# Two graph layers on one core: layernorm scaling and GAT slope on ScalarE, whole runs of weighted sums, packed loads, a second GAT block beside the first, and a timed instruction order

## Chip, cores and metric

One core of one Trainium2 chip. The metric is the device time of one execution in microseconds (us), median of the runs. TensorE is "PE" in the profile, its weight load "PEld", VectorE "DVE", ScalarE "ACT", GpSimd "POOL". SBUF is the on-chip memory that all engines use, PSUM the one that TensorE writes its results to.

## The reference, cut to what matters

128 graphs of 128 nodes with 256 features pass through two layers, all in fp32.

```python
# layer 0: two graph-attention (GAT) blocks, then a feed-forward
def _gat(h, adj, W, a):
    Wh = h @ W
    e = leaky_relu(Wh @ a[:F] + swapaxes(Wh @ a[F:], 1, 2), 0.2)
    att = softmax(where(adj > 0, e, NEG), axis=1)
    return att @ Wh
h = layernorm(x + gat(gat(x)))            # g, b
h = layernorm(h + relu(h @ wf1 + bf1) @ wf2 + bf2)
# layer 1: 8 heads, 4 relations; each relation r weighs its own values
attn = softmax(q @ k.T / sqrt(32))
out = sum((attn * (adj == r)) @ v_r for r in range(4))
x = layernorm(h + out @ Wo + bo)
x = layernorm(x + gelu(x @ W1 + b1) @ W2 + b2)
```

In the data every gain is 1 and every bias 0. The kernels compute with them all the same.

## The kernel before

It works on groups of four graphs, 32 groups. Each group has five stages (load, GAT, feed-forward 0, attention, feed-forward 1), written as Python generators. A loop takes the steps of many groups in turn by a nominal time, so that one group's attention stands beside another's feed-forwards. The program is then put in order for each engine by a scheduler that follows this sequence, and each engine executes its own list in order.

```python
def layernorm(y, k):                     # all on VectorE but the power
    for b in range(G):
        nc.vector.bn_stats(st, y[:, b]); nc.vector.bn_aggr(mv[:, b], st)
    nc.vector.tensor_scalar(rstd, mv[:, :, 1], EPS, None, op0=OP.add)
    nc.gpsimd.tensor_tensor(rstd, rstd, mhalf, OP.pow)
    g, beta = ln[k]                      # rows, the same in all partitions
    for b in range(G):
        nc.vector.scalar_tensor_tensor(y[:, b], y[:, b], mv[:, b, 0:1], g, op0=OP.subtract, op1=OP.mult)
    for b in range(G):
        nc.vector.scalar_tensor_tensor(y[:, b], y[:, b], rstd[:, b:b + 1], beta, op0=OP.mult, op1=OP.add)

def feed_forward(h, ...):
    hT = transposed(h)                   # PE transposes, copies by ACT and DVE
    yield
    nc.gpsimd.tensor_add(y, h, over_graphs(bout))     # bias of its second product, 128x1024
    # ... cut: matmuls, eviction with the activation on ACT, second matmuls

def gat_weighting(wh, c, cap):
    # ... cut: four PE transposes into p
    nc.vector.tensor_tensor(e, p, wh[:, :, c:c + 1].to_broadcast([P, G, N]), OP.add)
    nc.vector.scalar_tensor_tensor(e, e, ALPHA, e, op0=OP.mult, op1=OP.max)
    nc.vector.scalar_tensor_tensor(e, cap, BIG, e, op0=OP.subtract, op1=OP.min)
    # ... cut: row maximum, four Exp on ACT, reciprocal, product on POOL

def weighted(ms, v):                     # "av": 32 matmuls, 32 output rows each
    for c in range(DC):
        for r in range(R):
            for q in range(HC):
                nc.tensor.matmul(po[ts(q, DH), c], v[:, r, ...], ms[c][r][:, q],
                                 start=r == 0, stop=r == R - 1, tile_position=(0, q * DH))

# loads: first group, then weights; 25 of them, 18 small vectors and 7 pieces of matrices, are issued by ACT
stages = ((stage_load, 1, -0.7, -0.6), (stage_gat, 6, 0.0, 0.5), (stage_ff0, 7, 0.65, 1.15),
          (stage_attention, 15, 2.0, 3.0), (stage_ff1, 7, 3.15, 3.65))   # steps, begin, end
```

Names in the lines below: `tr` is a transpose into PSUM, `T` its copy in SBUF, `mm` any other product, `wh` the GAT projection, `e` the weights of a GAT block or of attention, `kbd` the keys as the score product reads them, `v` the values, `m` the masked weights, `av` the weighted sum, `cap` the GAT mask, `fT` the hidden layer of a feed-forward. Each fp32 matmul shows as two instructions.

## Time and profile before

3866.5 us. Cut by the first wq matmul of each group, the profiled execution is:

| stretch | us | floor of TensorE's work in it | idle of TensorE, up to its last matmul |
|---|---|---|---|
| start, up to the second group's wq | 243.6 | 149.6 | 67.4 |
| 28 full periods, mean | 117.5 | 107.5 | 5.1 |
| the rest | 332.7 | 282.8 | 24.5 |

"Floor" is the sum of the start-to-start times that each kind of matmul has in an unbroken run (0.43 us for 512 columns, 0.216 for 256, 0.109 for a transpose, 1.89 for the 64 instructions of an av block), worked out as the prediction tells.

In the start, ScalarE's first work waited for its own load issues, and the GAT chain ran alone. From the timeline of the kernel before (start, length, engine, line, operation, count, idle before and releaser):

```profile
27.35 1.28 ACT L236 ACT_TABLE_LOAD   x1 [27.35 <-DMA wv<-in_wv_dram]
```

```profile
40.32 3.81 PE L244 MATMUL mm<-wh,e 128*128 128x258 f32 x8 [9.93 <-POOL e L224]
...
50.88 3.69 PE L253 MATMUL mm<-wh,e 128*128 128x256 f32 x8 [5.97 <-POOL e L224]
59.31 2.11 PE L160 MATMUL tr<-ident,tok 128*128 128x128 f32 x8 [4.74 <-issue]
61.67 15.43 PE L193 MATMUL mm<-T,wf 128*128 128x512 f32 x32 [0.25 <-ACT T L164]
```

Each GAT matmul waits for a chain over DVE, ACT and POOL; the first feed-forward (L193) begins at 61.7 us.

### The profile page before, as it was taken

Reading aid. Unit: us, or ns where it says so; the run is one execution under the profiler, and the core shown is the slowest. Engines: PE = TensorE matmul, PEld = TensorE weight load, DVE = VectorE, ACT = ScalarE, POOL = GpSimd, SP = SyncE. Lnnn points to the kernel's source line nnn. Section 1 sums busy time; section 2 is a strip of 40 time slices with the busy share of each in tenths; the row PEclk is TensorE's granted clock in tenths of the full one; section 3 lists DMA queues with packets and bytes.
Section 4 is the critical chain, followed back from the end, with each engine's and each line's share of the span. In section 5 each row is a group of like instructions: output and inputs, shape, how many; then the busy total and the mean of one; then the engine's idle time right before and its main releaser. Section 6 shows DMA issues by size and latency. Waiting matters only on the chain.

```text
span 3866.8 us, 51771 instructions
## 1 busy us (share of the span) xinstructions
PE 3623.2 (94%) x20240; PEld 2329.2 (60%) x20240; DVE 2236.5 (58%) x4804; ACT 1509.9 (39%) x4272; POOL 722.4 (19%) x552
## 2 busy tenths in 40 slices
PE   5799999999999999999999999999999999999998
PEld 3456666566565665666665656665656665656655
DVE  2466565655656556555666565566565566565654
ACT  1243444434444334453334443334443334443342
POOL 0121111211112112111111122111122111122111
PEclk8899999999999999999999999999999999999999
DMA  4000000000000000000000000000000000000000
GB/s 160 8 9 20 14 17 9 20 20 15 20 6 20 20 15 20 6 20 20 20 14 20 6 20 20 20 14 20 6 20 20 20 15 14 6 9 6 6 7 11
DMA packets 28884, 70.83 MB, mean 18 GB/s; under 512 B 5600, under 2 KB 11616, under 8 KB 28640
## 3 DMA queue, kind: packets, MB, share of 16 engines
q1 hardware_dynamic: 21328, 63.19, 4.7%
q10 hardware_dynamic: 7312, 4.34, 0.4%
q8 instruction: 159, 2.61, 0.3%
q14 instruction: 85, 0.70, 0.1%
HBM read 50.74 MB, written 16.78 MB: 17 GB/s over the span
## 4 chain that ended last, share of the span: by engine, by line
PE 68%; DVE 17%; ACT 9%; issue 3%; POOL 2%; DMA 1%; ACTq 0%; POOLq 0%; DVEq 0%; SPq 0%
PE mm L203 22%; PE mm L193 17%; PE mm L319 6%; DVE m L310 5%; PE av L330 4%; DVE tok L181 3%; ACT kbd L280 3%; PE mm L287 3%; PE mm L266 3%; PE mm L353 2%; PE mm L244 2%; PE mm L276 2%; PE tr L306 2%; PE mm L235 1%; PE tr L160 1%
## 5 line engine op out<-in xcount | busy, mean ns | idle before, releaser
L310 DVE SCALAR_TENSOR_TENSOR m<-at,tr 128x512 f32<-128x512 int32 x1024 | 631.0, 680 | 5.8 <-PE tr L306 5.1
L204 DVE TENSOR_TENSOR tok<-tok,mm 128x512 f32<-128x512 f32 x128 | 88.0, 687 | 781.8 <-PE mm L203 781.8
L319 PE MATMUL mm<-wv,T 128*128 128x512 f32 x1024 | 479.8, 603 | 0.0
L193 PE MATMUL mm<-T,wf 128*128 128x512 f32 x1024 | 469.3, 600 | 6.8 <-DVE T L162 6.3
L193 PE MATMUL mm<-T,w 128*128 128x512 f32 x1024 | 470.0, 602 | 2.0 <-ACT T L164 0.5
L293 ACT ACTIVATE e<-mm,nm 128x128 f32<-128x128 f32 x1024 | 360.3, 372 | 266.0 <-DVE nm L289 162.6
L203 PE MATMUL mm<-w,fT 128*128 128x256 f32 x2048 | 455.5, 381 | 0.0
L203 PE MATMUL mm<-wf,fT 128*128 128x256 f32 x2048 | 452.4, 379 | 0.0
L203 PEld LDWEIGHTS mm<-w,fT 128*128 128x128 f32 x2048 | 386.6, 190 | 71.1 <-issue 21.5
L203 PEld LDWEIGHTS mm<-wf,fT 128*128 128x128 f32 x2048 | 386.7, 190 | 51.3
L295 POOL TENSOR_TENSOR e<-e,s 128x512 f32<-128x512 f32 x256 | 276.9, 1082 | 702.6 <-DVE s L294 700.0
L176 POOL TENSOR_TENSOR rstd<-rstd,mhalf 128x4 f32<-128x4 f32 x128 | 150.9, 1179 | 1369.9 <-DVE rstd L175 1369.9
L280 ACT ACTIVATE kbd<-mm,bk 32x256 f32<-32x256 f32 x512 | 238.3, 465 | 376.2 <-PE mm L276 365.0
L181 DVE SCALAR_TENSOR_TENSOR tok<-tok,rstd,lnb 128x256 f32<-128x256 f32 x512 | 292.9, 624 | 104.6 <-POOL rstd L176 104.6
L195 ACT ACTIVATE fT<-mm,bf 128x512 f32<-128x512 f32 x256 | 175.4, 694 | 413.1 <-PE mm L193 412.0
L193 PEld LDWEIGHTS mm<-T,wf 128*128 128x128 f32 x1024 | 192.2, 191 | 229.4 <-issue 203.1
L193 PEld LDWEIGHTS mm<-T,w 128*128 128x128 f32 x1024 | 191.3, 193 | 230.1 <-issue 205.1
L330 PEld LDWEIGHTS av<-m,v 128*32 128x32 f32 x8192 | 219.0, 109 | 155.4 <-issue 99.9
L330 PE MATMUL av<-m,v 128*32 128x128 f32 x8192 | 286.5, 275 | 13.7 <-DVE v L320 13.4
L287 PE MATMUL mm<-kbd,T 128*128 128x512 f32 x512 | 257.8, 606 | 24.0 <-ACT kbd L280 24.0
L319 PEld LDWEIGHTS mm<-wv,T 128*128 128x128 f32 x1024 | 183.6, 194 | 158.9 <-issue 158.5
L289 DVE TENSOR_REDUCE nm<-mm 128x4 f32<-128x512 f32 x256 | 173.5, 683 | 175.6 <-PE mm L287 175.6
(65 smaller groups left out, 4243.0 us busy)
## 6 DMA issues: line engine op xcount, KB each, us to landing
xt<-in_xT_dram SPq DMA_DIRECT2D x32, 512.0 KB, 3.3
tok<-in_x_dram SPq DMA_DIRECT2D x32, 512.0 KB, 3.2
out_dram<-tok SPq DMA_DIRECT2D x32, 512.0 KB, 2.6
at<-in_adjT_dram SPq DMA_DIRECT2D x32, 256.0 KB, 2.6
wf<-in_wf_dram SPq DMA_DIRECT2D x2, 1024.0 KB, 8.9
w<-in_w_dram SPq DMA_DIRECT2D x2, 1024.0 KB, 9.3
wv<-in_wv_dram ACTq DMA_DIRECT2D x2, 512.0 KB, 9.9
lng<-in_g_dram ACTq DMA_DIRECT2D x4, 128.0 KB, 6.0
```

What stands on the lines that cost most here:

```text
L181: nc.vector.scalar_tensor_tensor(y[:, b], y[:, b], rstd[:, b:b + 1], beta, op0=OP.mult, op1=OP.add)
L193: nc.tensor.matmul(p, win[:, c, ts(f, P)], hT[:, c], start=c == 0, stop=c == DC - 1)
L195: nc.scalar.activation(t, p, func, bias=bin_[:, f:f + 1])
L203: nc.tensor.matmul(p[:, b - b2_], fT[f][:, ts(b, N)], wout[:, f], start=f == 0, stop=f == FC - 1)
L280: nc.scalar.activation(kbd[c][rows, :, q], p[rows], AF.Identity, bias=bk[rows, c:c + 1])
L287: nc.tensor.matmul(p, qT[:, c, ts(b, N)], kbd[c][:, b % KG], start=True, stop=True)
L289: nc.vector.tensor_reduce(nm, p, AX.X, OP.max, negate=True)
L293: nc.scalar.activation(e[:, q], p[:, q], AF.Exp, bias=nm[:, q:q + 1], accum_out=s[:, q:q + 1])
L295: nc.gpsimd.tensor_mul(e, e, per_row(s, N))
L310: nc.vector.scalar_tensor_tensor(m, ab, r, pT, op0=OP.is_equal, op1=OP.mult)
L319: nc.tensor.matmul(p, hT[:, f, ts(b, N)], wv[:, f, r:r + 2], start=f == 0, stop=f == DC - 1)
L330: nc.tensor.matmul(po[ts(q, DH), c], v[:, r, c * P + q * DH:c * P + (q + 1) * DH], ms[c][r][:, q], start=r == 0, stop=r == R - 1, tile_pos ...
```

## The change

The intent: relieve VectorE, keep the narrow matmuls together, and shorten the start.

```diff
-    # bcast(), cols(): one small load for each vector, on nc.scalar's queue
+    # COLS, rows: all vectors packed into `cols` and `rows`; every load on nc.sync,
+    # in the order M, W2T, xT[0], W1T, adj[0], x[0], cols, wf1, rows, wf2, ... w2, then group 1
     # normalised(), was layernorm()
-        for b in range(G):  # two VectorE passes with row vectors g, beta
-            nc.vector.scalar_tensor_tensor(... subtract mean, times g)
-            nc.vector.scalar_tensor_tensor(... times rstd, plus beta)
+        nc.vector.scalar_tensor_tensor(nmr, mv[:, :, 0], -1.0, rstd, op0=OP.mult, op1=OP.mult)
+        for b in range(G):
+            nc.scalar.activation(y[:, b], y[:, b], AF.Identity, bias=nmr[:, b:b + 1], scale=rstd[:, b:b + 1])
+    def affine(y, k, b):     # gain, then offset with the next bias, two graphs at a time, off the path
+        for op, v in zip((OP.mult, OP.add), ln[k][0]):
+            nc.gpsimd.tensor_tensor(y[:, b:b + 2], y[:, b:b + 2], v[:, None, :].to_broadcast([P, 2, D]), op)
     # transposed(): gain and offset go into the copies, where they are per partition
-                nc.vector.tensor_copy(t[:, c], p)
+                nc.vector.tensor_scalar(t[:, c], p, gain[:, c:c + 1], offset[:, c:c + 1], op0=OP.mult, op1=OP.add)
     # gat_weighting()
+        for b in range(G):
+            nc.scalar.activation(p[:, b], p[:, b], AF.Prelu, bias=wh[:, b, c:c + 1], alpha=ALPHA)
-        nc.vector.tensor_tensor(e, p, wh..., OP.add)
-        nc.vector.scalar_tensor_tensor(e, e, ALPHA, e, op0=OP.mult, op1=OP.max)
-        nc.vector.scalar_tensor_tensor(e, cap, BIG, e, op0=OP.subtract, op1=OP.min)
+        nc.vector.scalar_tensor_tensor(e, cap, BIG, p, op0=OP.subtract, op1=OP.min)
     # weighted(): last mask first, so the first matmul's wait covers all, and a higher priority
-            for c in range(DC):
-                for r in range(R):
+            with tc.high_priority(offset=200):
+                for c in reversed(range(DC)):
+                    for r in reversed(range(R)):
     # attention(): keys(b + 1) one step earlier; every yield now has a share of its stage's time
-        att = gat_weighting(wh, D + 2, cap)
-        yield
+        att = gat_weighting(wh, D + 2, cap)
+        yield 4
+            if g == 1 and n < 2:         # the second group's load and GAT beside the first's
+                begin, end = begin - 0.6, end - 0.6
-    with tile.TileContext(nc) as tc:
+    with tile.TileContext(nc, schedule_with_timeline_sim=True) as tc:
```

The last line hands the order of instructions to a scheduler that works with estimated durations ("timed scheduler" below).

## The prediction

> **What bounds the kernel now.** I read the page first, then busy time by stage, the order of work on TensorE inside one stage, and what the other engines did in its gaps. From the page, busy time, share of the span and instruction count:
>
> ```profile
> PE 3623.2 (94%) x20240; PEld 2329.2 (60%) x20240; DVE 2236.5 (58%) x4804; ACT 1509.9 (39%) x4272; POOL 722.4 (19%) x552
> ```
>
> TensorE (PE) is the bound; the others have 40% or more to spare on average. So work moved between VectorE, ScalarE and GpSimd can only help through the idle 243 us of TensorE, and through time in which it is "busy" but stretched.
>
> Stage table. The first wq matmul of each group of four graphs (L266) marks a period. Columns: window, length, busy time by engine (PE, weight load, DVE, ACT, POOL), granted clock, DMA share, GB/s.
>
> ```profile
> 150.76:243.55 92.79, 84.84 (x529) 53.59 (x528) 59.56 (x130) 33.06 (x118) 19.35 (x15) 0.98 0.03 9
> 243.55:359.60 116.05, 111.25 (x634) 71.55 (x633) 70.33 (x150) 46.35 (x133) 22.60 (x17) 1.00 0.05 17
> 359.60:480.10 120.50, 114.99 (x634) 74.02 (x633) 70.04 (x150) 49.29 (x135) 22.60 (x17) 0.97 0.05 16
> 480.10:598.70 118.60, 113.14 (x634) 73.09 (x633) 70.06 (x150) 49.30 (x135) 22.60 (x17) 0.99 0.05 16
> 3739.30:3867.00 127.70, 106.61 (x585) 64.70 (x583) 57.67 (x131) 38.88 (x107) 17.72 (x14) 0.95 0.02 9
> ```
>
> The kernel is a start of 150.8 us, one short period of 92.8, 29 like periods up to 3648.4 (mean 117.4; either 116.0 at clock 1.00, or 120.5 and 118.6 in turn at 0.97 and 0.99), and an end of 90.9 + 127.7. The reader is to see that equal work costs up to 4.5 us more where the clock dips.
>
> One undisturbed period on TensorE (start, length, line, operation, count, idle before it and its releaser):
>
> ```profile
> 2605.81 3.60 PE L266 MATMUL mm<-T,wq 128*128 128x512 f32 x8
> ...
> 2610.97 7.07 PE L203 MATMUL mm<-wf,fT 128*128 128x256 f32 x32
> 2617.88 1.92 PE L235 MATMUL mm<-wx,xt 128*128 128x260 f32 x8
> ...
> 2626.34 0.65 PE L213 MATMUL tr<-ident,wh 128*128 128x128 f32 x4 [2.24 <-DVE T L162]
> ...
> 2629.84 0.65 PE L306 MATMUL tr<-ident,e 128*128 128x128 f32 x4 [1.31 <-POOL e L295]
> ...
> 2661.15 0.84 PE L330 MATMUL av<-m,v 128*32 128x128 f32 x18
> 2662.45 1.13 PE L287 MATMUL mm<-kbd,T 128*128 128x512 f32 x2 [0.45 <-ACT kbd L280]
> 2663.50 0.64 PE L330 MATMUL av<-m,v 128*32 128x128 f32 x16
> ...
> 2691.71 1.95 PE L330 MATMUL av<-m,v 128*32 128x128 f32 x64
> ```
>
> Start-to-start rates of unbroken runs give a floor: 32 at 256 columns take 6.91 us (0.216 each), those of 512 columns 0.43, a transpose 0.109, the 64 narrow av matmuls 1.89. Times the counts of a period: two feed-forwards 55.1, values 13.7, scores 6.9, q and k 6.9, wo 3.5, av 7.6, GAT 7.0, transposes 7.0: **107.5 us**. The clean period is 116.0, so 8.5 us are lost: 4.8 idle, 3.7 stretched.
>
> The longest wait is DVE's copy L162. What DVE and POOL did ahead of it:
>
> ```profile
> 2622.46 2.34 POOL L188 TENSOR_TENSOR tok<-tok,b 128x1024 f32<-128x1024 f32 x1 [0.97 <-PE tr L160]
> 2622.53 2.56 DVE L181 SCALAR_TENSOR_TENSOR tok<-tok,rstd,lnb 128x256 f32<-128x256 f32 x1
> ...
> 2625.61 0.68 DVE L162 COPY T<-tr 128x512 f32<-128x512 f32 x1
> ```
>
> One layernorm instruction whose median is 0.48 us took 2.56, for as long as POOL's bias add. Everything behind it on DVE slid, the T copy too, and TensorE stood still.
>
> **What the Trainium skill says.** "SBUF — State Buffer", section "Who interferes with whom": a DVE instruction with two SBUF inputs contends with a GpSimd instruction that reads SBUF, as an exclusive lock for the whole instruction; with at most one SBUF input (outside two-port modes) it does not. The trace agrees: L181 reads tok and lnb from SBUF and has 447/480/2566 ns as minimum, median, maximum. "TensorE: Matmul & The Clock Gate", Part 1, says the clock halves after low activity in a window of about 3.4 us; the 0.97 and 0.99 periods agree in kind. "ScalarE: Activation LUTs", "What ACT_TABLE_LOAD costs": 1283 ns a load, which the trace shows exactly (1283), 186 ns plus 0.833 per element for an ACTIVATE, some 93 ns for each pointer operand, and about 93 ns overlap between neighbours. "Trainium Kernel Development and Optimization", "Key Constraints": loads issued from several engines share the same 16 DMA engines. In the first 50 us they were 90% busy at 302 GB/s, so one queue loses no bandwidth; it frees ScalarE's sequencer, whose first copy had waited until 27.35 us behind its own load issues.
>
> **The change, part by part.** (Counts from the built kernel's order of instructions.)
>
> 1. *Matmul work:* counts are identical, so the floor of 107.5 stays.
> 2. *DVE.* Removed: both layernorm passes (292.9 + 267.9 us) and two of the three GAT passes (43.6 + 51.4) = 655.8. Added: 128 tiny products (21) and slightly dearer transpose copies (7). 2236 becomes about 1610 us. More important: the remaining full-width DVE operations read one operand from PSUM or have one SBUF input, so the lock should disappear from DVE.
> 3. *ACT.* Added: 512 scalings of 256 elements, about 0.46 us each back to back (estimate from L280, 465 ns, and the ScalarE page's pointer and overlap terms) = 235; 256 Prelu of 128 elements at about 0.3 = 80; dearer transpose copies 17. Table loads fall from 208 to 184, −31. 1510 becomes about 1810 (50%). Not a bound.
> 4. *POOL.* Removed: 96 bias adds, 225.7. Added: 512 operations on 128x512 at about 1.08 (row L295 has 1082 ns on that size) = 553. 722 becomes 1050 (29%). These sit on residual data, off the path to the next matmul, since gain and offset go into the transpose copies.
> 5. *Order on TensorE.* The 32-matmul av blocks (64 instructions) become unbroken, keys are issued earlier, and a timed scheduler fixes the rest.
>
> Taken back from the clean period's 8.5: the T wait 2.4, the POOL wait before L306 1.5, the GAT matmul waiting and running slow (L244) 1.1, broken av runs with their kbd waits 1.5: 6.5. The remaining 2.0 is about 0.1 us at each change of matmul kind, which stays. That makes 109.5 at best; I choose **111.0**, adding 1.0 for new waits of an in-order ScalarE or POOL with more to do and 0.5 for clock dips. 29 × (117.4 − 111.0) = 186 us.
>
> *Start.* The chain of waits there is serial GAT work, twice: TensorE waits 11.9, 6.6, 9.9, 6.0, 4.7 in group 0 and 8.6, 6.1, 4.6 in group 1. Now M, W2T, xT and W1T come first (1.3 MB, some 4 us at 302 GB/s plus 2 of latency); the first GAT can run about 10 us sooner. But the second group's xT is queued behind all weights: 10.6 MB, about 37 us, and its projection stands ahead of group 0's last GAT matmul. So group 0's feed-forward starts at about 53 us, not 61.7. From there to the first wq, 58 us of work is dense: 3% for changes and 3 for a cold clock make 62. First wq at **115** instead of 150.8: −36. The next stretch has similar gaps to lose: 92.8 to **87**, −6.
>
> *End.* The last feed-forward has no neighbour. The final normalisation gains two POOL operations per half after ScalarE, partly overlapped: about +4. The attention before it loses its broken av runs, −3.5. 218.6 becomes **219**.
>
> Sum: 115 + 87 + 29 × 111.0 + 219 = 3640 us, 5.9% shorter.
>
> **Rivals.** (a) *ScalarE becomes the wait.* One normalisation is now four scalings of 0.46 in an in-order stream that also holds eight kbd writes (3.9 us in a row), feed-forward evictions and table loads. With four mm buffers, TensorE would stall at L193 or L287. For it: kbd already shows as a releaser. Against: 50% load, and a stream ordered for it. Two such waits of 1.5 us a period make 114, total near 3725. (b) *POOL, with the lock now against itself or with 2.2 us pairs in front of the attention product L295.* POOL already held 2.35 us operations, so I expect no more; at 1 us in each of four graphs it would be 115, total 3755. (c) *TensorE is the bound and the waits merely move.* Then only start and clock are gained: near 3800. Against it: L213's and L306's waits have named causes which the change removes. (d) *Everything works and clock dips vanish:* 109.3, total near 3590.
>
> **Range and chances.** The period decides: 109.0 to 113.3 with the start ±8 gives 3580 to 3710. Within 2% needs a period above 116, that is, (c) or (a) and (b) together: 3.5%. Slower by 2% would need 8 us of new waits in each period: 0.5%.
>
> **What would show it.** Right: periods of 110 to 112; no idle before the GAT transposes put down to DVE's T copy; no DVE instruction stretched to about 2 us; av only in runs of 64; DVE near 1610, ACT 1810, POOL 1050 busy; first feed-forward matmul near 53 and a wait for the second group's xT just before. Wrong: new idle before feed-forward or score matmuls released by ACT normalisation or kbd; POOL operations far over 1.1 us; a start not below 135; more clock dips than before.

## More of the kernel before

Every kernel was timed against the kernel before on the same chip, and the kernel before gave 3866 to 3871 us on each of the chips used; variants that ran on different chips are compared through it.

## The result

3662.8 us (3661.6 to 3665.2, 4 runs) against 3867.5 us. The ratio is 0.9471 (95% interval 0.9454 to 0.9487). A ratio is the mean time of one kernel's fast runs over that of the other's in the same rounds, so it is not quite the ratio of the medians quoted. The range 3580 to 3710 held.

The page of the changed kernel, its engine line:

```profile
PE 3526.9 (96%) x20240; PEld 2315.1 (63%) x20240; DVE 1735.9 (47%) x3781; ACT 1827.3 (50%) x5016; POOL 1094.9 (30%) x968
```

Busy time by stretch, same columns as in the prediction:

```profile
0.00:108.69 108.69, 85.30 (x296) 59.65 (x297) 25.72 (x64) 38.96 (x99) 24.67 (x27) 0.91 0.40 144
108.69:197.81 89.12, 82.57 (x531) 53.99 (x530) 49.11 (x106) 40.06 (x135) 22.41 (x20) 0.98 0.03 10
1092.56:1204.10 111.54, 109.38 (x635) 71.82 (x634) 54.72 (x119) 57.46 (x157) 33.94 (x31) 1.00 0.05 17
2212.64:2324.97 112.33, 109.56 (x635) 71.95 (x633) 54.24 (x119) 57.34 (x158) 34.23 (x30) 1.00 0.05 17
3529.32:3660.20 130.88, 106.25 (x585) 66.05 (x583) 45.94 (x103) 47.06 (x123) 33.43 (x30) 0.93 0.02 9
```

One period on TensorE, its idle times and av blocks:

```profile
2228.12 3.70 PE L202 MATMUL mm<-T,w 128*128 128x512 f32 x8 [0.43 <-ACT T L190]
...
2245.11 1.95 PE L341 MATMUL av<-m,v 128*32 128x128 f32 x64
...
2254.66 3.70 PE L328 MATMUL mm<-wv,T 128*128 128x512 f32 x8 [0.52 <-ACT fT L204]
...
2273.60 7.17 PE L214 MATMUL mm<-w,fT 128*128 128x256 f32 x32 [1.08 <-ACT e L302]
```

In this period the waits on DVE's T copy and on POOL's product are gone; over the whole run the wait before the GAT transposes is no longer listed, and the one for POOL's product fell from 31.0 to 5.3 us. Every av run has 64 instructions, and what idle time is left is mostly released by ScalarE. The clock is 1.00 in both periods; in the kernel before, a mean period (117.5) is 1.5 us longer than one at full clock (116.0), so part of what a period gained is clock.

Where the 206.6 us between the two profiled executions went: the start fell from 243.6 to 197.8 (−45.7), 28 full periods from 117.52 to 112.08 (−152.4), the rest from 332.7 to 324.2 (−8.5).

### The profile page after: what moved, and what is told of

The parts are those of the page before. It is cut to its first block, busy times and chain, and to the rows that moved or that the text cites. A ratio compares the mean times of both kernels' runs of the same rounds, so it can differ in the third digit from the quotient of the medians.

```text
span 3660.2 us, 51841 instructions
## 1 busy us (share of the span) xinstructions
PE 3526.9 (96%) x20240; PEld 2315.1 (63%) x20240; DVE 1735.9 (47%) x3781; ACT 1827.3 (50%) x5016; POOL 1094.9 (30%) x968
## 4 chain that ended last, share of the span: by engine, by line
PE 73%; ACT 15%; DVE 8%; POOL 1%; issue 1%; DMA 1%; POOLq 0%; ACTq 0%; SPq 0%; DVEq 0%
PE mm L214 22%; PE mm L202 18%; PE mm L328 10%; PE av L341 5%; DVE m L319 3%; ACT e L302 3%; PE mm L246 3%; PE mm L296 3%; PE mm L285 3%; PE mm L277 2%; ACT L204 2%; PE mm L366 2%; PE tr L315 2%; ACT e L233 2%; ACT L302 2%; ACT fT L204 2%
## 5 line engine op out<-in xcount | busy, mean ns | idle before, releaser
L177 POOL TENSOR_TENSOR tok<-tok,ln_rows 128x512 f32<-128x512 f32 x512 | 643.5, 1283 | 623.1 <-PE tr L186 572.6
L304 POOL TENSOR_TENSOR e<-e,s 128x512 f32<-128x512 f32 x256 | 266.2, 1044 | 995.7 <-DVE s L303 792.5
L204 ACT ACTIVATE fT<-mm,col 128x512 f32<-128x512 f32 x512 | 340.2, 692 | 421.5 <-PE mm L202 420.3
L328 PE MATMUL mm<-wv,T 128*128 128x512 f32 x1024 | 467.9, 596 | 14.9 <-ACT fT L204 14.9
L171 ACT ACTIVATE tok<-tok,nmr,rstd 128x256 f32<-128x256 f32 x512 | 265.5, 596 | 174.8 <-DVE nmr L169 174.7
L328 PEld LDWEIGHTS mm<-wv,T 128*128 128x128 f32 x1024 | 187.9, 191 | 213.3 <-issue 175.1
L289 ACT ACTIVATE kbd<-mm,col 32x256 f32<-32x256 f32 x512 | 238.6, 466 | 151.5 <-PE mm L285 144.8
L202 PEld LDWEIGHTS mm<-T,wf 128*128 128x128 f32 x1024 | 183.6, 190 | 199.5 <-issue 176.4
L341 PE MATMUL av<-m,v 128*32 128x128 f32 x8192 | 251.2, 275 | 13.9 <-DVE v L329 12.4
L167 POOL TENSOR_TENSOR rstd<-rstd,mhalf 128x4 f32<-128x4 f32 x128 | 130.0, 1016 | 396.1 <-DVE rstd L166 328.8
L296 PE MATMUL mm<-kbd,T 128*128 128x512 f32 x512 | 241.5, 593 | 1.7 <-ACT kbd L289 1.4
```

Of the source, the lines that this page charges most:

```text
L171: nc.scalar.activation(y[:, b], y[:, b], AF.Identity, bias=nmr[:, b:b + 1], scale=rstd[:, b:b + 1])
L177: nc.gpsimd.tensor_tensor(y[:, b:b + 2], y[:, b:b + 2], v[:, None, :].to_broadcast([P, 2, D]), op)
L202: nc.tensor.matmul(p, win[:, c, ts(f, P)], hT[:, c], start=c == 0, stop=c == DC - 1)
L204: nc.scalar.activation(t, p, func, bias=bin_[:, f:f + 1])
L289: nc.scalar.activation(kbd[c][rows, :, q], p[rows], AF.Identity, bias=bk[rows, c:c + 1])
L296: nc.tensor.matmul(p, qT[:, c, ts(b, N)], kbd[c][:, b % KG], start=True, stop=True)
```

## The experiments

What remained open is which part did it. A period lost its named waits, but several parts could each have taken them. Theory W: the parts that relieve VectorE took them away. Rival S: the order did. Here is every run; "period" is the mean of its 28 full periods. Every variant under the timed scheduler also gets an order of its own, so a difference between two of them is that of the part together with the order made for it.

| kernel | us | ratio to before | start | period | rest |
|---|---|---|---|---|---|
| before | 3867 | 1 | 243.6 | 117.52 | 332.7 |
| changed | 3662.8 | 0.9471 | 197.8 | 112.08 | 324.2 |
| sched_only | 3866.7 | 0.9995 | 261.8 | 116.90 | 330.1 |
| no_sched | 3988.9 | 1.0314 | 198.8 | 122.88 | 347.6 |
| pool_writes | 3792.1 | 0.9802 | 244.3 | 114.96 | 327.1 |
| av_forward | 3684.7 | 0.9527 | 194.7 | 113.00 | 325.4 |
| no_sched_no_affine | 3705.6 | 0.9577 | 196.5 | 113.55 | 327.7 |
| sched_av | 3952.9 | 1.0216 | 261.9 | 119.51 | 341.3 |
| slope_dve | 3637.3 | 0.9401 | 199.7 | 111.10 | 324.4 |
| no_beside | 3685.9 | 0.9526 | 220.8 | 112.07 | 325.5 |
| ln_dve | 3719.2 | 0.9614 | 209.5 | 113.61 | 326.9 |
| scale_dve | 3718.3 | 0.9611 | 204.0 | 113.25 | 341.7 |
| ends_slope | 3629.1 | 0.9381 | 192.3 | 111.10 | 323.4 |
| sched_av_placed | 3739.3 | 0.9663 | 250.0 | 112.78 | 329.6 |

### Is the lock real? (pool_writes)

```diff
-        nc.gpsimd.tensor_add(y, h, over_graphs(bout))       # and the same with bo
+        scr = wk.tile([P, 2, D], F32, name="scr", bufs=1)
+        nc.gpsimd.tensor_copy(scr[:, 0, :G], h[:, :, 0])
+        for _ in range(5):
+            nc.gpsimd.memset(scr, 0.0)
```

> The kernel before, its three POOL bias adds per group (biases are zero here, so the output stays right) replaced by a 4-element copy and five memsets of 128x512: POOL is as long busy at the same place but reads almost nothing from SBUF. Lock theory (a VectorE instruction with two SBUF inputs waits for a POOL instruction that reads SBUF): the layernorm instructions lose their 2.5 us maximum (below 1.5 us, from other POOL products), the 2.24 us wait of the GAT transposes on the T copy shrinks below 0.5 us, period 113 to 114.5, total 3775 to 3825. Rival (VectorE is simply late, because two layernorm passes stand before the T copy in its queue): the maximum stays where POOL is busy or the wait stays above 1.5 us, total 3845 to 3870.

75 us faster (ratio 0.9802, interval 0.9788 to 0.9817): clear of noise. The same layernorm instruction, its shortest, median and longest time in ns, before and in pool_writes:

```profile
L181 DVE SCALAR_TENSOR_TENSOR tok<-tok,rstd,lnb x512: 447/480/2566, 58.7 to 3862.7; 128x256 f32<-128x256 f32 x171
L181 DVE SCALAR_TENSOR_TENSOR tok<-tok,rstd,lnb x512: 453/479/1262, 59.7 to 3786.0; 128x256 f32<-128x256 f32 x171
```

And the wait of the GAT transposes (total us, times, longest), before and in pool_writes:

```profile
PE tr L213 <- DVE T L162: 65.1, 29, 2.3
PE tr L216 <- DVE T L162: 0.5, 3, 0.2
```

The longest fell from 2566 to 1262 ns while POOL was busy for longer in total (761 against 722 us). Nothing was taken from VectorE, so its backlog alone was not the cause. But the expectation's "at the same place" did not hold: none of the memsets ran beside any of the 512 L181 instructions. The run shows what the bias adds cost where they stood, and does not by itself tell reading from writing. What names the lock is the trace of the kernel before, instruction by instruction: of 30 L181 that ran beside a bias add 29 took 2556 to 2566 ns and one, which had begun 0.13 us before the add, 479 (the add then took 2557 in place of 2345); the 447 with POOL idle took 467 to 489; and the copy L162, whose one input is in PSUM, took 680 to 693 beside a bias add and 651 to 679 with POOL idle. In pool_writes all L181 over 486 ns stand beside the attention product, which reads SBUF on POOL.

So in the kernel before, three POOL bias adds a group cost 2.6 us a period: 1.9 in periods at full clock (116.0 to 114.1), the rest in fewer periods at a lower clock. The period of 114.96 is 0.5 above the range expected; other waits grew, that for the values before av from 13.4 to 26.4 us in all.

### The timed scheduler, with and without the parts (sched_only, no_sched)

```diff
 # sched_only: the kernel before
-    with tile.TileContext(nc) as tc:
+    with tile.TileContext(nc, schedule_with_timeline_sim=True) as tc:
 # no_sched: the changed kernel, the opposite edit
```

> The kernel before with the timed scheduler and nothing else. Theory W (the named waits were taken away by the parts: DVE relieved, lock gone, av runs whole): the scheduler alone brings little, since VectorE still carries both layernorm passes and POOL's 2.35 us bias adds still stretch them: period 114 to 116, total 3780 to 3850, DVE instructions of layernorm still with a maximum near 2.5 us. Rival S (the order of instructions did it, the parts are decoration): period near 112, total 3680 to 3730.

> The changed kernel with the timed scheduler taken out and all parts kept. Theory W: most of the gain stays, period 112.5 to 114.5, total 3680 to 3750. Rival S: most of the gain is lost, period above 115.5, total above 3790.

Neither theory fits. The scheduler alone brought nothing (ratio 0.9995, interval 0.998 to 1.001): 17 us less in 28 periods, 18 us more in the start. The parts without it made the kernel 3.1% slower than before. The gain is in neither; it needs both. In sched_only the long T wait is gone, but av was torn further (346 runs in place of 236, down to 2 instructions), with new waits for values and masks. In no_sched the reason stands in POOL's timeline, with TensorE's below it:

```profile
1569.87 4.92 POOL L177 TENSOR_TENSOR tok<-tok,ln_rows 128x512 f32<-128x512 f32 x4 [3.00 <-PE tr L186]
1574.76 1.04 POOL L304 TENSOR_TENSOR e<-e,s 128x512 f32<-128x512 f32 x1
1575.75 1.02 POOL L167 TENSOR_TENSOR rstd<-rstd,mhalf 128x4 f32<-128x4 f32 x1
```

```profile
1575.85 1.12 PE L315 MATMUL tr<-ident,e 128*128 128x128 f32 x4 [5.84 <-POOL e L304]
```

Four gain-and-offset passes stand together in front of the attention product and the layernorm power. The passes are needed by nobody soon, but an engine takes its list in order. This was the prediction's rival (b), and it becomes true as soon as the order isn't made for it. TensorE's clock fell to 0.96 in such a period.

### Taking those passes away (no_sched_no_affine)

```diff
     def affine(y, k, b):
-        for op, v in zip((OP.mult, OP.add), ln[k][0]):
-            nc.gpsimd.tensor_tensor(...)
+        return           # right only because gains are 1 and offsets 0 here
```

> The changed kernel in program order (no timed scheduler, 3989 us) with the POOL gain-and-offset passes dropped (gain is 1 and offset 0 in this data, so the output stays right; it isn't a legal change). POOL theory (in program order four passes of 1.23 us stand in a row before the attention product that TensorE waits for, 5.84 us a period, and before the rstd power): that wait goes, and the wait on the GAT projection copies shrinks; period 122.8 to between 114 and 117, total 3730 to 3810. Rival (the order of TensorE or ScalarE is at fault): period above 119, total above 3870.

The period fell from 122.9 to 113.55, a little below the range expected. In program order, POOL's sixteen passes cost 9.3 us a period, about 3 of it in lower clock and stretched matmuls (TensorE's idle time fell by 6.4). The wait before L315 was halved, from 188.8 to 90.4 us in all; it did not go, as was expected. Under the timed scheduler the kernel has all the passes and still takes only 112.08. By this reckoning what the scheduler does for the changed kernel is mostly to keep them out of the way; the changed kernel without them was not run, so this is not shown directly. The kernel is not a legal change, since it drops the gains.

### Whole av runs (av_forward, sched_av)

```diff
 # av_forward: the changed kernel        # sched_av: the opposite, on sched_only
-            with tc.high_priority(offset=200):
-                for c in reversed(range(DC)): ...
+            for c in range(DC): ...      # start=r == 0, stop=r == R - 1
```

> The changed kernel with the weighted sums in forward order and ordinary priority, as before. Theory (whole runs save 0.7 to 1.5 us a period): av shows again in runs of fewer than 64, period 112.5 to 113.4, total 3683 to 3715. Rival (the keys, issued earlier, were the gain; or the timed scheduler keeps the runs whole anyway): 3655 to 3670.

22 us slower, as expected by the theory at its lower end; order and priority were taken back together. A period of av_forward, two of its av runs, and the av line of one period in the changed kernel and in av_forward (count, busy us):

```profile
2115.64:2228.64 113.00, 112.20 (x634) 71.58 (x633) 54.27 (x120) 57.27 (x157) 34.19 (x30) 1.00 0.05 17
```

```profile
2149.87 0.41 PE L340 MATMUL av<-m,v 128*32 128x128 f32 x2
2152.12 1.50 PE L340 MATMUL av<-m,v 128*32 128x128 f32 x42
```

```profile
L341 PE MATMUL av<-m,v 128*32 128x128 f32 x256 | 7.8, 274 | 0.4 <-DVE v L329 0.4
L340 PE MATMUL av<-m,v 128*32 128x128 f32 x256 | 10.0, 277 | 0.0
```

Two narrow instructions by themselves take 0.41 us, 64 in a run take 1.9 (from the run's start to the start of the next matmul, medians of 0.34 and 1.88). TensorE is idle for only 0.8 us a period here, less than in the changed kernel (2.6), and 98% busy over the whole span, yet slower. Torn runs hide as busy time; the Trainium skill's first page ("Trainium Kernel Development and Optimization", "Performance Expectations") says that matmul busy time is a bad measure of how near a kernel is to its limit, and this pair shows it.

> The kernel before with the timed scheduler and the weighted sums reversed and prioritised, nothing else. Theory (the scheduler alone gained the T wait and lost as much by tearing the av blocks into runs of 2 to 16): period 116.7 to between 113 and 115, total 3760 to 3820, av in runs of 64. Rival (torn runs cost nothing, the loss lies in VectorE's lateness): period above 116, total above 3840.

This expectation failed: with whole runs the old kernel became 2.2% slower than before, not faster. Its waits tell where (releaser, us in total, times, longest):

```profile
PE mm L244 <- POOL e L224: 93.5, 32, 7.6
PE mm L287 <- ACT kbd L280: 65.7, 64, 1.2
PE av L331 <- DVE v L320: 52.8, 31, 2.7
```

Every period the GAT matmul waits for its weights and the score matmul for its keys. TensorE's idle time rose from 4.2 us a period in sched_only to 8.1, and the clock of the full periods fell from 1.00 to 0.98. It looks as if torn av runs had been filling these gaps; the next run tests the placing.

### The placing of steps (sched_av_placed)

```diff
 # on sched_av: the changed kernel's shares of time and early keys, nothing else
         att = gat_weighting(wh, D + 2, cap)
-        yield
+        yield 4
+            if b + 1 < G and (b + 1) % KG == 0:
+                keys(b + 1)
             yield 1
             if b + 1 < G:
-                if (b + 1) % KG == 0:
-                    keys(b + 1)
                 es = weights(b + 1)
     # ... cut: the other shares, and the stages' totals 11, 8.5, 16, 8.5
```

> sched_av (3953 us, which my expectation missed) plus the placing of the changed kernel: its shares of time for each step (four after a GAT weighting in place of one) and the keys issued a step earlier. Layernorm, GAT slope, POOL bias adds of 2.35 us and loads stay as before. Placing theory (sched_av lost its 8 us a period because GAT products and keys stood too close behind their producers): the waits on the GAT product (2.9 us) and on kbd (2.1 us a period) go, period 119.3 to between 113.5 and 115.5, start near 158, total 3775 to 3835. Rival (VectorE, late and locked by POOL, can't feed whole av runs): period above 117.5, total above 3890.

The period fell from 119.5 to 112.8, 0.7 below the expected range, and the total of 3739 is 36 below. The two waits named went: 9.8 us in all are left before L244 and 1.1 for kbd. A period of it:

```profile
2507.95:2620.43 112.48, 109.58 (x634) 71.80 (x633) 70.76 (x152) 46.60 (x134) 22.68 (x17) 1.00 0.05 17
```

VectorE is as busy as in the kernel before (70.8 us a period), both layernorm passes and the GAT slope are on it, POOL's bias adds are there in one piece, and some layernorm passes still take up to 2197 ns. Even so the period is within 0.7 us of the changed kernel's 112.08. Of the 5.44 us that a period gained, 4.74 come from order alone: timed scheduler, whole runs, shares and early keys together. The moves of arithmetic, added last, bring 0.70 more. Of the total of 205 us, order alone gives 128; most of the other 77 is in the start (250.0 to 197.8).

### The moves of arithmetic (ln_dve, scale_dve, slope_dve)

```diff
 # ln_dve: changed kernel, both layernorm passes of the kernel before, plain transpose copies,
 #         next bias added by POOL two graphs at a time
 # scale_dve:
-            nc.scalar.activation(y[:, b], y[:, b], AF.Identity, bias=nmr[:, b:b + 1], scale=rstd[:, b:b + 1])
+            nc.vector.tensor_scalar(y[:, b], y[:, b], rstd[:, b:b + 1], nmr[:, b:b + 1], op0=OP.mult, op1=OP.add)
 # slope_dve: the kernel before's add, max and min on VectorE in place of Prelu and min
```

> The changed kernel with the layernorm of the kernel before on VectorE (two passes with row vectors, plain transpose copies, the next bias added by POOL in halves); order, scheduler, GAT slope, packed loads stay. Theory (VectorE's relief is what the rest of the change rests on): about 560 us of two-SBUF-input passes come back to VectorE and meet POOL's reads again; period 114.5 to 118, total 3740 to 3850. Rival (the timed order hides them: VectorE would be at 62%): period below 112.8, total below 3695, or faster since ScalarE and POOL are relieved.

3719 us: the period is 1.5 us longer, the start 11.7. Less than theory W asked, more than the rival. Layernorm on ScalarE is worth 56 us here, but the rest of the change does not rest on it.

> The changed kernel with only the scaling by mean and rstd moved from ScalarE to VectorE, as one pass with one SBUF input and two column operands. ScalarE theory (its in-order stream, 50% busy, releases most of TensorE's remaining waits, and slope_dve gained 0.97 us a period by freeing 88 us of it): freeing 265 us gains 0.5 to 1.5 us a period, total 3620 to 3650. Lock theory (the pass runs in a two-port mode, as cap does with 417 to 1516 ns, and POOL's 1.28 us passes stretch it): its maximum is over 1.2 us, total 3655 to 3720.

55 us slower, at the upper end of the lock theory's forecast. The pass in scale_dve:

```profile
L171 DVE TENSOR_SCALAR tok<-tok,rstd,nmr x512: 395/408/1376, 44.9 to 3708.0; 128x256 f32<-128x256 f32 x171
```

One SBUF input did not protect it: 308 of these with POOL idle took 395 to 414 ns, 204 beside POOL up to 1376. So the lock is there, but it isn't what the full periods lost. They lost 33 us (the start 6, the end 17.5), and TensorE's idle time in them rose by 27.0 us, of which 26.4 stand before one matmul, the values product L328, which waits for a feed-forward eviction on ScalarE (0.51 us a time in the changed kernel):

```profile
PE mm L328 <- ACT fT L204: 41.6, 29, 1.7
```

ScalarE loads the table for an exponential 12.6 us ahead of it. The load in the changed kernel, then in scale_dve:

```profile
1792.73 1.28 ACT L302 ACT_TABLE_LOAD   x1
1701.72 1.28 ACT L302 ACT_TABLE_LOAD   x1 [0.94 <-DVE nm L298]
```

The maximum nm is not late: it starts 1.06 us after the score product L296 in both. In scale_dve the exponential waits for two semaphores, VectorE's and GpSimd's, and VectorE's wait stands before the table load; in the changed kernel there is one wait, behind the load. All 29 waits of over 1.4 us before L328 follow such a load; in all, 30 loads of the changed kernel have no wait before them, and every such load of scale_dve but two has one. The run ln_dve shows the same wait before L328 (41.5 us). What the lock cost in the start and the end was not taken apart.

> The changed kernel with the GAT slope back on VectorE (add, then max of 0.2x and x), Prelu gone. Theory A (VectorE's relief there matters little: it is 47% busy, and add plus max take as long as four Prelus, 1.4 against 1.5 us): 3650 to 3675. Theory B (ScalarE is the tighter engine of the two now, 50% and the releaser of most waits): faster, 3625 to 3650. Theory C (two-input passes meet POOL's lock again): slower, 3680 to 3720, with a maximum of such a pass near 1.9 us.

Theory B held: with the slope back on VectorE the kernel takes 3637 us, 0.98 us less a period. One part of the change costs 25 us. The Prelus (88.9 us in all, four to a GAT weighting) stood in ScalarE's list. The 0.52 us wait for the feed-forward eviction (14.9 us in all) is no longer among TensorE's waits in slope_dve, and in the changed kernel two Prelus stand ahead of that eviction; the other differences are too small to name one cause for the rest.

### The start (no_beside) and a version that beats both (ends_slope)

```diff
 # no_beside: changed kernel
-            if g == 1 and n < 2:
-                begin, end = begin - 0.6, end - 0.6
 # ends_slope: slope_dve, and
     wf1 = wload("wf1")
+    second_load = load_group(1)          # was behind all the weights
-            affine(y, "12", b)
+            affine(y, "12", b, nc.vector if g == NG - 1 and b == 0 else nc.gpsimd)
```

> The changed kernel without the earlier placing of the second group's GAT. Theory (it fills the gaps of the first one's chain): the first wq matmul moves from 108.7 to between 118 and 130 us, total 3672 to 3690. Rival (the timed scheduler fills the gaps anyway, or the second group's xT behind all the weights eats the gain): first wq within 5 us, total 3655 to 3668.

The start grows from 197.8 to 220.8, the rest stays. So the earlier second GAT is worth 23 us. The other 23 of the start's 46 (220.8 against 243.6) belong to packed loads, a free ScalarE and the other parts together; no run separates them, but with layernorm back on VectorE the start is 11.7 longer (ln_dve). The start in the changed kernel:

```profile
32.08 6.22 PE L246 MATMUL mm<-wx,xt 128*128 128x260 f32 x16 [4.89 <-DMA xt<-in_xT_dram]
...
45.83 1.18 PE L186 MATMUL tr<-ident,tok 128*128 128x128 f32 x4 [5.36 <-ACT tok L171]
...
52.39 10.47 PE L202 MATMUL mm<-T,wf 128*128 128x512 f32 x24
```

The second group's projection waits for a load that lies behind all the weights, and the first group's last GAT matmul stands behind it in TensorE's list.

> The candidate: slope_dve plus the second group's three loads queued right after the first weights, plus half of the last gain-and-offset pass on VectorE. Theory: the 4.9 us wait for xT goes and what follows it on the chain moves up; first wq from 109.9 to between 100 and 105, end 2 to 3 us shorter, period as in slope_dve (110.8); total 3620 to 3632. Rival (the first feed-forward waits for other loads or for the serial GAT chain): first wq above 107, total 3632 to 3640.

3629.1 us, ratio 0.9381, 0.9% less than the changed kernel and 0.2% less than slope_dve. The intervals of the last two ratios overlap (0.9367 to 0.9395 and 0.9387 to 0.9415); what tells them apart is the profile, a start of 192.3 in place of 199.7 at the same period. The load wait is gone and the feed-forward begins earlier:

```profile
46.58 11.70 PE L203 MATMUL mm<-T,wf 128*128 128x512 f32 x24
```

The first wq matmul comes at 104.2 us in place of 109.9, the end is 1.0 us shorter (323.4 against 324.4), less than the 2 to 3 expected.

## Why the prediction was right, point by point

The total was 23 us above the predicted 3640, well inside the range. That it came so near is in part luck: by stretch, the first wq came 6.3 us earlier than forecast, the next stretch took 2.1 more (89.1 for 87), 29 periods 24 more, the end 0.6 more (20 in the profile's span of 3660.2; the device time of 3662.8 holds 2.6 outside it).

- **Bound and floor.** Held: matmuls and their rates are unchanged, the work of a full period is 107.5 in both. (The terms that the prediction lists add up to 107.7.)
- **The period.** Predicted 111.0 over 29 periods, measured 111.8 (112.08 over the 28 full ones). The waits that it named went. Over the floor, 2.0 us are stretched work, as forecast, and 2.6 are idle, of which ScalarE releases most; the allowance of 1.0 for new waits was too small.
- **What takes the waits away.** Here a step failed: the prediction gave the gain to VectorE's relief and the vanished lock, and called the order a remainder ("a timed scheduler fixes the rest"). The lock is real and cost 2.6 us a period (pool_writes), but placing removes the same waits with lock and VectorE load in place (112.8 in sched_av_placed). Two remedies for one wait, and the sum came out near because it was counted once.
- **The GAT slope.** Counted as a gain for VectorE; measured as a loss of 0.98 us a period (slope_dve).
- **VectorE's sum.** About 1610 predicted, 1736 measured. The lock did not disappear, it moved to instructions that the sum held to be tiny: nmr reads two inputs in SBUF, and took 149 to 165 ns in the 48 cases with POOL idle, 571 to 1231 in the 80 others. In the changed kernel (ns, shortest, median, longest):

```profile
L169 DVE SCALAR_TENSOR_TENSOR nmr<-mv,rstd x128: 149/579/1231, 44.8 to 3650.0; 128x4 f32<-128x4 f32 x128
```

  The 128 products were put at 21 us and took 85.7; rstd went from 20.8 to 50.3 and cap from 13.7 to 27.5. That is 108 of the 126 us.
- **ScalarE.** 1810 against 1827. The term for 512 scalings was 235, measured 265.5: L280's 465 ns, one pointer operand more and one overlap less gave 0.46; an instruction takes 588 and overlaps the one before by 95, so 492 back to back, and the first of each four overlaps nothing of its own kind.
- **POOL.** 1050 against 1095. A pass takes 1.28 us, not the 1.08 of the product of the same size.
- **The start.** First feed-forward at 53 predicted, 52.4 measured. The predicted wait for xT (4.9 us) is there, but at 32.1, before the second group's projection; the last long wait before the feed-forward is one of 5.4 for ScalarE's layernorm scaling. First wq at 115 predicted, 108.7 measured: the remaining work was put at 58 us plus 5, and 56 passed in all.
- **The end.** 219 against 219.6.
- **Rivals.** (a) is what is left of the waits, at a small size. (b) did not happen in the changed kernel and did in no_sched, at 9.3 us a period. (c) did not: the period fell at an unchanged clock too, from 116.0 to 112.1. (d) came half true: the clock dips are gone from the periods.
- **Slower by 2%.** The prediction says that this needs 8 us of new waits a period; by its own sum it is 10.5 (a period of 121.5). The changed parts without the timed scheduler got there (122.88).

## What to carry to other kernels

When a wait has two possible remedies, a lighter producer or a better place in the order, try the order first and by itself: here 4.7 of 5.4 us a period came from it, and one of the moved operations cost time. In the start the other parts did most. Before giving an in-order engine work that nobody waits for, look at what stands behind it in the list; sixteen such passes, four in a row in places, cost 9 us a period in program order, and with all of them the timed order is still 1.5 us shorter than program order without any. When an undone part costs time, follow the wait that grew to its releaser before blaming the part: in scale_dve it was a table load behind a semaphore wait. A part that is bad alone (whole runs: +2.2% without the placing) can be good in company, so undo parts from the finished kernel as well as adding them to the old one.

## What the Trainium skill lacked or had wrong

- "SBUF — State Buffer", "Who interferes with whom": right on two-input passes (2556 to 2566 ns behind a bias add that began first, 467 to 489 with POOL idle) and on a single-input `tensor_scalar`, which by that page can enter a two-port mode (408 ns median, 1376 longest in scale_dve). It says nothing of size: a 128x4 product of two SBUF inputs takes 579 ns in the median and 1231 at the longest, against 149 free. And not every POOL instruction that reads SBUF holds VectorE up: in the kernel before, 157 passes L179 ran beside the 1.2 us power of 128x4 and took 471 to 482 ns, against 447 to 486 with POOL idle.
- "ScalarE: Activation LUTs", "Rules for kernel authors", sends multiplication and addition to VectorE. For the GAT slope that was right (25 us); for the layernorm scaling it did not pay here (scale_dve is 55 us slower, 26 of them behind one table load): the rule is one per element and knows neither POOL's lock nor what else stands in the engine's list. The page's cost formula ("What ACT_TABLE_LOAD costs") fits: 585 ns for 256 elements with two pointer operands, 588 measured.
- "TensorE: Matmul & The Clock Gate", Part 3, tells what packed narrow matmuls gain, not what a torn run costs: two instructions alone took 0.41 us, 64 together 1.9. ("TensorEngine Tiling (Array Packing)", "Key Properties", says that a change of mode drains the engine, without a time.)
- I found no page that tells that a table load can stand behind a semaphore wait of the activation that it serves: 0.94 us later in scale_dve than in the changed kernel, in every full period.
- I found no page that tells how a POOL tensor_tensor depends on the layout of its second operand: 1276 ns with a row vector repeated over two graphs, 1040 with one value repeated along each row, both 128x512.
